# A graph network's count matrices: the first block read early into a buffer of its own, fewer tests on the counts, later tests on the lists

## The chip, the cores and the metric

The kernel runs on one core of one Trainium2 chip. The core has a matrix engine (PE, called TensorE), a vector engine (DVE), a scalar engine (ACT), a general engine (POOL), a queue engine that only issues transfers (SP), and 16 DMA engines that carry every transfer. The five instruction streams run side by side and wait for one another through semaphores. The metric is the device time of one execution in microseconds (us), as the median of several runs; lower is better.

## The reference

Two message-passing layers on a graph of 6250 nodes with 128 features and 200,000 edges sorted by target node. Cut to what matters:

```python
h = relu(layernorm(x))
agg_src  = segment_sum(h[src], dst, 6250)          # a node's sum over the sources of its edges
agg_edge = segment_sum(edge_attr_128, dst, 6250)
x = x + relu(concat([h, agg_src, agg_edge]) @ W.T + b)          # layer 0

h = relu(layernorm(x))
mean(h) = segment_sum(h[src], dst) / max(degree, 1)
h   = relu(mean(h) @ W1_l + b1 + h @ W1_r)                      # layer 1
out = relu(mean(h) @ W2_l + b2 + h @ W2_r)                      # layer 2
x = x + out
```

The targets are drawn as 6250 times the square of a uniform number, so the low node numbers have by far the most edges.

## The kernel before, in words

**Counts in place of gathers.** The kernel never gathers rows. It builds, once, the matrix of how many edges lead from each source to each target, and then each of the three layers is a product of that matrix with a table of features. The nodes are cut into NB = 49 blocks of 128. For a target block `b`, the counts are a tile `c` of 128 x (128 x 49) bf16 numbers, 1568 KB. They lie in DRAM in `counts_d`, block after block. The product for one target block is 49 matmuls, one for each source block, which accumulate in one PSUM tile `ps`. The table of features, `terms`, holds each number as a sum of three bf16 parts (NK = 3), so one matmul moves 384 columns, 385 in layer 0, where a column of ones counts the degree.

**The build (lines 486 to 587).** The edges come in 196 groups of 1024, in order of target. For each group DVE makes one-hot matrices (`sp`, `sq`, line 391), PE multiplies them (lines 534 and 546) and ACT puts the result in one of three ring buffers in SBUF (line 561). When a stretch of groups is done, SP writes the ring to `counts_d` (line 584, up to 1004 KB). The place of the write comes from the data, so two writes may overlap, and each waits until the one before has landed; the number of stretches is NS. Between these, PE also sums the edge features (line 437, into `aggE`, from `edge_t`, read on SP's queue at line 426) and multiplies the normed inputs by the weights of layer 0 (`products`, lines 336 to 352). At the end the build's buffers are released, and the pools `late` (tests, second table `terms1`), `loads` (three buffers of `c`) and `psum` take their place.

**The layers (lines 598 to 775).** `neighbours(layer, b)` reads `c` (line 603, SP's queue), multiplies (line 609; in layer 0 also `aggE` by `we_sb`, line 608), makes `rdeg`, one over the degree, in layer 0 (lines 611 and 612) and adds the three parts to `y` (line 620). In layers 0 and 1 the block's row of the next layer's table follows. In layer 0 that is the sum with `own` (line 740), the residual (741), the norm (326 to 334), and then, as in layer 1, a transpose `pt` on PE (line 341), a product `pz` (line 344) and the rounding into three parts (345 to 351). The table for the next layer must be whole before a block of that layer can finish, but its first 48 of 49 matmuls don't need the last block. A planner in the framework places each engine's instructions in one fixed order, from its own estimate of times; so `pt` of block b stands among the matmuls of block b + 1 at a place fixed in advance, and PE waits there if `h` isn't ready.

**The tests.** The fast path holds only for inputs that fit its windows, so the kernel tests them and computes all again in a slow, general way (`general`) if a test fails. There are three kinds. (1) No count may exceed 255, since bf16 holds integers exactly only so far: for each block, DVE takes the maximum of two halves of `c` (line 617) and reduces it (line 618); the even blocks do it in layer 0, the odd ones in layer 1. `worse` collects the results. (2) `windows_right` (lines 632 to 714) loads the list of targets twice, `both` and `nexts` (about 784 KB each, on POOL's queue), and tests windows and order on DVE; nothing but its loads holds these back. (3) Within it are tests on small tables, `rows` and `limits`: `limits` goes to DRAM and back (lines 660 and 662). `all_right` combines all in layer 2.

Of the kernel before, what the change touches and what calls it, by code (L numbers as in the profile page):

```python
# [9 lines left out]
F32 = mybir.dt.float32  # L10
F16 = mybir.dt.float16
BF16 = mybir.dt.bfloat16
I32 = mybir.dt.int32
AF = mybir.ActivationFunctionType
ALU = mybir.AluOpType
AX = mybir.AxisListType
# [4 lines left out]
P = 128  # L21
D = 128
# [6 lines left out]
NK = 3  # L29
# [27 lines left out]
def kernel(ctx: ExitStack, tc: tile.TileContext, x, srcl, dstl, edge, w0t, b0, w1l, b1, w1r, w2l, b2, w2r, out):  # L57
# [11 lines left out]
    nc = tc.nc  # L69
    N = x.shape[0]  # L70
    E = edge.shape[0]
    NB = -(-N // P)
# [16 lines left out]
    for g0, g1, *reg in regions:  # L89
        for g in range(g0, g1, reg[2]):  # L90
            stretches.append((g, min(reg[2], g1 - g), *reg))
    NS = len(stretches)

    dram = ctx.enter_context(tc.tile_pool(name="dram", bufs=1, space=bass.MemoryType.DRAM))
    counts_d = dram.tile([P, (NP + SWMAX) * NB], BF16, name="counts_d")
# [13 lines left out]
    work = fast.enter_context(tc.tile_pool(name="work", bufs=2))  # L109
    keep = fast.enter_context(tc.tile_pool(name="keep", bufs=1))  # L110
# [7 lines left out]
    rdeg = const.tile([P, NB], F32, name="rdeg")  # L118
    worse = const.tile([P, 6 + NC], F32, name="worse")
    bad = const.tile([1, 8], F32, name="bad")  # L120
    first = const.tile([P, 2, G], F32, name="first")
    terms = [keep.tile([P, NB, TW], BF16, name="terms0")]
    aggE = keep.tile([P, NP + WINMAX], F32, name="aggE")

    build = ExitStack()
    lists = build.enter_context(tc.tile_pool(name="lists", bufs=1))
# [8 lines left out]
    steps = lists.tile([1, GU - T1], F32, name="steps")  # L135
    seam_i = lists.tile([1, NS], I32, name="seam_i")
    NQ = max(w for _, _, _, w, *_ in regions) * NB
# [9 lines left out]
    far = once.tile([P, GU], F32, name="far")  # L147
    starts, seam, most = (once.tile([1, NS], F32, name=name) for name in ("starts", "seam", "most"))
    q_n = once.tile([P, GU], F16, name="q_n")
# [13 lines left out]
    si = 0  # L163
    for g0, g1, n, w, k, sw, win in regions:
        nc.gpsimd.memset(room[:, g0:g1], float(sw - w))
        m = -(-(g1 - g0) // k)
# [94 lines left out]
    for z, lay in ((p_n, p_e), (q_n, q_e)):  # L261
        for s0 in range(0, U, 2):
            pt = spsum.tile([P, 2, 256], F32, name="pt", bufs=2)
            for s in range(2):
                for u in range(U):
                    c = P * (s0 + s) - u + U - 1
# [11 lines left out]
    si = 0  # L278
    while si < NS:
        g0, k = stretches[si][:2]  # L280
        m = 1
        while si + m < NS and stretches[si + m][1] == k:
            m += 1
        units = unit[:, g0 : g0 + m * k].rearrange("o (m j) u -> o m (j u)", j=k)
        nc.vector.tensor_copy(starts[:, si : si + m], units[:, :, 0])
        if si == 0:
# [5 lines left out]
            op=ALU.subtract,  # L292
# [6 lines left out]
    nc.vector.memset(seam[:, 0:1], 0.0)  # L299
    nc.vector.tensor_tensor(seam[:, 1:], starts[:, 1:], starts[:, : NS - 1], op=ALU.subtract)  # L300
    nc.vector.tensor_tensor(seam[:, 1:], seam[:, 1:], most[:, : NS - 1], op=ALU.min)
    nc.vector.tensor_scalar(seam, seam, 0.0, float(NB), op0=ALU.max, op1=ALU.mult)
# [7 lines left out]
    for end, u in ((0, 0), (GU + 1, GU - 1)):  # L310
# [5 lines left out]
    nc.vector.tensor_scalar(  # L316
        bad[:, 1:2], starts[:, NS - 1 : NS], -1.0, float(NC * P - stretches[-1][5]), op0=ALU.mult, op1=ALU.add
    )
    setup.close()
    nc.gpsimd.memset(terms[0][:, :, NK * D :], 1.0)  # L320

# [56 lines left out]
    def value(ap, engine, most):  # L378
        return nc.values_load(
            ap, engines=[engine], min_val=0, max_val=most, skip_runtime_bounds_check_because="clamped on the chip"  # L380
        )
# [39 lines left out]
    def edge_sums(g):  # L421

        win = win_of(g)
        e = edges.tile([P, U, D], F32, name="edge_t")
        at_e = min(g * EG, E - EG)
        nc.sync.dma_start(e, edge[at_e : at_e + EG, :].rearrange("(p u) f -> p u f", u=U))
        hot = padded[g % len(padded)]
        nc.vector.tensor_tensor(  # L428
            hot[:, :, :win],
            iota[:, :win].unsqueeze(1).to_broadcast([P, U, win]),  # L430
            rel[:, g, :].unsqueeze(2).to_broadcast([P, U, win]),
            op=ALU.is_equal,
        )
        ps = bpsum.tile([P, 512], F32, name="pe", bufs=2)
        for u in range(U):
            behind = yield
            mm = nc.tensor.matmul(ps[:, :P], e[:, u, :], hot[:, u, :], start=u == 0, stop=u == U - 1)  # L437
            if behind is not None:
                tc.add_manual_dep(mm.ins, behind.name, IN_ORDER, reason="in turn with the counts")
        base = value(first_i[0:1, g : g + 1], ET.DVE, N - 1)  # L440
        to = aggE[:, bass.ds(base, win)]
        nc.vector.tensor_tensor(to, to, ps[:, :win], op=ALU.add)

    def all_edge_sums():
        for g in range(G):
            yield from edge_sums(g)

    edge_tiles = all_edge_sums()
    next(edge_tiles)
    summed = 0  # L450
# [42 lines left out]
    block = 0  # L493
    for i in range(2):
        load_chunk(i)
    for si, (g0, ng, n, w, k, sw, win) in enumerate(stretches):
        nq = NB * w
        ring = ring_of[si % 3]
# [5 lines left out]
        for g in range(g0, g0 + ng):  # L504
# [21 lines left out]
            for j in range(0, len(live), many):  # L526
                units = live[j : j + many]
                pu = bpsum.tile([P, 2 * 512], F32, name="pu", bufs=3)
                for i, t0 in enumerate(units):
                    for t in range(t0, t0 + n):  # L530
                        c = i * 512
                        while c < i * 512 + nq:
# [8 lines left out]
                            c = z  # L541
# [17 lines left out]
                for i, t0 in enumerate(units):  # L559
# [4 lines left out]
                    add = nc.gpsimd.tensor_tensor(to, to, fore[:, i, :], op=ALU.add)  # L564
# [15 lines left out]
        if si == 0:  # L580
            begin = 0
        else:
            begin = value(first_i[0:1, g0 : g0 + 1], ET.SP, N - 1) * NB
        nc.sync.dma_start(counts_d[:, bass.ds(begin, sw * NB)], ring[:, : sw * NB])
        before = ring
    assert block == NB and summed == GU and not writes
    build.close()
# [4 lines left out]
    loads = fast.enter_context(tc.tile_pool(name="loads", bufs=3))  # L592
# [4 lines left out]
    def neighbours(layer, b):  # L597

        ps = psum.tile([P, 512], F32, name="ps", bufs=3)
        m = NK * D + (layer == 0)  # L600
        products = []
        c = loads.tile([P, P, NB], BF16, name="c")
        nc.sync.dma_start(c, counts_d[:, b * P * NB : (b + 1) * P * NB].rearrange("p (d k) -> p d k", k=NB))
        for k in range(NB):
            products.append((c[:, :, k], terms[layer % 2][:, k, :m]))
        for i, (stands, moves) in enumerate(products):
            if layer == 0 and i == 1:
                nc.tensor.matmul(ps[:, :D], aggE[:, b * P : (b + 1) * P], we_sb, start=False, stop=False)
            nc.tensor.matmul(ps[:, :m], stands, moves, start=i == 0, stop=i == len(products) - 1)  # L609
        if layer == 0:  # L610
            nc.vector.tensor_scalar(rdeg[:, b : b + 1], ps[:, m - 1 : m], 1.0, None, op0=ALU.max)
            nc.vector.reciprocal(rdeg[:, b : b + 1], rdeg[:, b : b + 1])
        if b % 2 == layer:
            half = P // 2 * NB
            cf = c.rearrange("p d k -> p (d k)")
            high = late.tile([P, half], BF16, name="high")
            nc.vector.tensor_tensor(high, cf[:, :half], cf[:, half:], op=ALU.max)  # L617
            nc.vector.tensor_reduce(worse[:, 6 + b : 7 + b], high, AX.X, ALU.max)  # L618
        y = work.tile([P, D], F32, name="y", bufs=3)
        nc.vector.tensor_reduce(y, ps[:, : NK * D].rearrange("p (k f) -> p f k", k=NK), AX.X, ALU.add)  # L620
        return y

    def next_layer(layer, b, h):
# [9 lines left out]
    def windows_right():  # L633

        both = late.tile([P, 2, GU], F32, name="both")
        dst, far = both[:, 0], both[:, 1]
        nc.gpsimd.dma_start(dst.bitcast(I32), dstl)
        nexts = late.tile([P, GU], I32, name="nexts")
        nc.gpsimd.memset(nexts[P - 32 :, GU - U :], PAD)
        nc.gpsimd.dma_start(nexts[: P - 1, :], dstl[1:, :])  # L640
        nc.gpsimd.dma_start(nexts[P - 1 :, : GU - U], dstl[0:1, U:])
# [94 lines left out]
    for b in order:  # L736
        xt = load_x(b)
        r = load_own(0, b)
        y = neighbours(0, b)
        nc.vector.tensor_tensor(y, y, r, op=ALU.add)  # L740
        nc.vector.scalar_tensor_tensor(xt, y, 0.0, xt, op0=ALU.max, op1=ALU.add)
        nc.scalar.dma_start(x1_d[b * P : (b + 1) * P, :], xt)
        next_layer(1, b, normed(xt))


    def sage(layer, b):
        r = load_own(layer, b)
        y = neighbours(layer, b)
        nc.vector.scalar_tensor_tensor(y, y, rdeg[:, b : b + 1], r, op0=ALU.mult, op1=ALU.add)  # L749
        return y  # L750

    tests = windows_right()
    for b in order:
        next(tests, None)
        y = sage(1, b)
# [4 lines left out]
    for b in order:  # L760
# [8 lines left out]
        y = sage(2, b)  # L769
# [233 lines left out]
```

## The time and the profile before

| | us |
|---|---|
| median of 3 runs | 2244.61 (2238.09 to 2248.94) |
| the profiled execution, whole | 2237.15 |
| its span, first to last instruction | 2235.4 |
| PE busy in the span | 2073.7 (93%) |
| DVE busy | 1242.0 (56%) |
| build, to the last matmul that belongs to it | 911.4 |
| first matmul of layer 0 | 928.3 |
| maximum tests on `c` (lines 617 and 618), 49 of each, DVE | 87.6 and 167.5 |

The span is what the trace covers; the execution's own time has 1.75 us more around it. A timeline line gives the start, the duration (of a merged run of equal instructions), the engine, the line, the operation and, in brackets, how long the engine was idle before and what ended that. An engine's name with q (SPq, ACTq, POOLq) means that it issues a transfer there. The profiled execution is 0.33% under the median of the three runs.

### The profile page before, as it was taken

The numbers are of one execution on the slowest core, as the hardware profiler recorded it, in microseconds if no ns is written. First come the engines' busy times: TensorE is split into PE (matmuls) and PEld (weight loads), VectorE is DVE, ScalarE is ACT, GpSimd is POOL, SyncE is SP. The second block draws the span as 40 slices with busy tenths as digits, with TensorE's granted clock in tenths as the row PEclk, the third lists the DMA queues.
The fourth block names the chain that finished last, engine by engine and source line by source line (L and its number), as shares of the span: only waits on it lengthen the run. The fifth ranks groups of instructions, "written<-read, shape, count | busy, mean of one in ns | idle before, by whom it ended". The sixth has DMA issues, their size and how long they took to land.

```text
span 2235.4 us, 38803 instructions
## 1 busy us (share of the span) xinstructions
PE 2073.7 (93%) x13717; PEld 1691.1 (76%) x13717; DVE 1242.0 (56%) x2419; ACT 789.2 (35%) x2011; POOL 205.0 (9%) x427
## 2 busy tenths in 40 slices
PE   6977778899999999689999999999999999999998
PEld 5865567677776677478878887788888888888887
DVE  8987776577777777465555554544444431111111
ACT  3465566688888889211111111111111110000000
POOL 4576650000000000100000000000000000000000
PEclk9999999999999999899999999999999999999999
DMA  3555566678888778745555555555555556666663
GB/s 121 179 191 173 193 221 233 217 266 280 281 301 300 283 293 291 280 167 205 205 194 203 206 205 189 190 194 206 192 190 201 202 187 227 226 226 227 227 226 135
DMA packets 147226, 488.20 MB, mean 218 GB/s; under 512 B 16017, under 2 KB 86735, under 8 KB 127312
## 3 DMA queue, kind: packets, MB, share of 16 engines
q1 hardware_dynamic: 88452, 456.84, 56.9%
q10 hardware_dynamic: 57996, 27.16, 4.2%
q8 instruction: 111, 1.82, 0.3%
q0 software_dynamic: 576, 1.63, 0.2%
q14 instruction: 91, 0.75, 0.1%
HBM read 362.19 MB, written 123.38 MB: 217 GB/s over the span
## 4 chain that ended last, share of the span: by engine, by line
PE 60%; ACT 13%; DMA 9%; DVE 8%; issue 6%; ACTq 2%; POOLq 0%; SPq 0%; POOL 0%; DVEq 0%
PE ps L609 44%; ACT ring L561 10%; PE pe L437 6%; PE pu L534 5%; DMA counts_d<-ring 4%; DMA c<-counts_d 3%; PE pz L344 2%; ACTq L384 1%; DMA edge_t<-in_edge 1%; DVE sq L391 1%; DVE worse L618 1%; PE pt L341 1%; DVE high L617 1%; ACT h L334 1%; DVE sp L391 1%
## 5 line engine op out<-in xcount | busy, mean ns | idle before, releaser
L609 PE MATMUL ps<-terms,c 128*128 128x384 bf16 (+1 forms) x7203 | 1226.7, 327 | 16.9 <-DMA c<-counts_d 16.9
L609 PEld LDWEIGHTS <-c 128*128 128x128 bf16 x7203 | 1019.9, 142 | 183.6 <-issue 21.7
L437 PE MATMUL pe<-hot,edge_t 128*128 128x128 f32 x3136 | 521.0, 294 | 33.5 <-DMA edge_t<-in_edge 17.1
L561 ACT CAST ring<-pu 128x490 f32 (+6 forms) x891 | 469.5, 534 | 96.9 <-PE pu L546 43.0
L437 PEld LDWEIGHTS pe<-hot,edge_t 128*128 128x128 f32 x3136 | 418.2, 195 | 70.2 <-issue 18.1
L534 PE MATMUL pu<-sq,sp 128*128 128x512 bf16 (+7 forms) x1782 | 387.0, 313 | 55.9 <-ACT ring L561 26.7
L391 DVE TENSOR_TENSOR sq<-iota,q_e 128x3136 bf16<-128x3136 f16 (+8 forms) x196 | 353.5, 1804 | 102.4 <-PE pu L546 83.2
L620 DVE TENSOR_REDUCE y<-ps 128x128 f32<-128x384 f32 x147 | 81.2, 552 | 383.3 <-PE ps L609 383.3
L534 PEld LDWEIGHTS <-sp 128*128 128x128 bf16 x1782 | 175.6, 100 | 99.4 <-issue 33.6
L564 POOL TENSOR_TENSOR ring<-ring,fore 128x49 f32 x280 | 161.8, 578 | 102.3 <-ACT fore L556 36.1
L618 DVE TENSOR_REDUCE worse<-high 128x1 f32<-128x3136 bf16 x49 | 167.5, 3419 | 1.6
L546 PE MATMUL pu<-sc,sp 128*128 128x49 bf16 x892 | 163.1, 186 | 0.0
L347 DVE TENSOR_TENSOR r<-pz,b_sb 128x128 f32<-128x128 f32 x98 | 28.6, 292 | 225.0 <-ACT terms L345 225.0
L391 DVE TENSOR_TENSOR sp<-iota,p_e 128x1024 bf16<-128x1024 f16 x196 | 135.4, 691 | 21.8 <-PE pu L534 16.9
L546 PEld LDWEIGHTS <-sp 128*128 128x128 bf16 x892 | 87.0, 98 | 70.2 <-issue 38.5
L566 ACT CAST ring<-pu 128x196 f32 (+5 forms) x280 | 112.3, 403 | 67.9 <-issue 39.5
L330 ACT ACTIVATE rstd<-mv,eps 128x1 f32<-128x1 f32 x98 | 29.5, 301 | 291.1 <-DVE mv L328 291.0
L757 ACT ACTIVATE h<-y 128x128 f32<-128x128 f32 x49 | 15.2, 309 | 281.0 <-DVE y L749 281.0
L617 DVE TENSOR_TENSOR high<-c 128x3136 bf16<-128x3136 bf16 x49 | 87.6, 1789 | 42.1 <-DMA c<-counts_d 42.1
L428 DVE TENSOR_TENSOR hot<-iota,rel 128x64 f32<-128x64 f16 (+13 forms) x196 | 96.5, 493 | 0.0
L351 DVE TENSOR_TENSOR terms<-z,terms 128x128 bf16<-128x128 f32 x147 | 43.9, 299 | 59.5 <-ACT terms L350 59.0
L350 ACT CAST terms<-z 128x128 bf16<-128x128 f32 x147 | 44.0, 299 | 76.4 <-DVE z L349 75.6
(144 smaller groups left out, 867.3 us busy)
## 6 DMA issues: line engine op xcount, KB each, us to landing
c<-counts_d SPq DMA_DIRECT2D x147, 1568.0 KB, 6.1
edge_t<-in_edge SPq DMA_DIRECT2D x196, 512.0 KB, 4.2
counts_d<-ring SPq DMA_DIRECT2D x21, 735.0 KB, 3.8
counts_d<-ring SPq DMA_DIRECT2D x14, 1004.5 KB, 5.4
counts_d<-ring SPq DMA_DIRECT2D x14, 931.0 KB, 4.7
counts_d<-ring SPq DMA_DIRECT2D x14, 882.0 KB, 4.6
counts_d<-ring SPq DMA_DIRECT2D x14, 833.0 KB, 4.9
own<-r_d ACTq DMA_DIRECT2D x147, 64.0 KB, 5.3
```

The costliest lines, as they stand in the source:

```text
L391: nc.vector.tensor_tensor(to.rearrange("p t (c two) -> p t c two", two=2), iota[:, :m].rearrange("p (c two) -> p c two", two=2).unsqueeze( ...
L428: nc.vector.tensor_tensor(hot[:, :, :win], iota[:, :win].unsqueeze(1).to_broadcast([P, U, win]), rel[:, g, :].unsqueeze(2).to_broadcast([P ...
L437: mm = nc.tensor.matmul(ps[:, :P], e[:, u, :], hot[:, u, :], start=u == 0, stop=u == U - 1)
L534: mm = nc.tensor.matmul(pu[:, c:z], sp[:, t, :], sq[:, t, c - i * 512 : z - i * 512], start=t == t0, stop=t == t0 + n - 1 and (n > 1 or c ...
L546: mm = nc.tensor.matmul(pu[:, i * 512 : i * 512 + NB], sp_b[:, t, :], sc[:, slot + 1 - len(last_tiles) + j0, :NB], start=False, stop=j0 == ...
L561: nc.scalar.copy(ring[:, bass.ds(to_put[t0], nq)], pu[:, i * 512 : i * 512 + nq])
L564: add = nc.gpsimd.tensor_tensor(to, to, fore[:, i, :], op=ALU.add)
L566: put = nc.scalar.copy(ring[:, bass.ds(to_put[t0 // n] + NB, nq - NB)], pu[:, i * 512 + NB : i * 512 + nq])
L609: nc.tensor.matmul(ps[:, :m], stands, moves, start=i == 0, stop=i == len(products) - 1)
L617: nc.vector.tensor_tensor(high, cf[:, :half], cf[:, half:], op=ALU.max)
L618: nc.vector.tensor_reduce(worse[:, 6 + b : 7 + b], high, AX.X, ALU.max)
L620: nc.vector.tensor_reduce(y, ps[:, : NK * D].rearrange("p (k f) -> p f k", k=NK), AX.X, ALU.add)
```

## The change

Line numbers in the text are those of the kernel before.

1. **A buffer for block 0's counts.** A tile `c_early` is taken for the whole run. The write of stretch NS - 7 is followed, on POOL's queue, by a load of block 0's counts into it, while the last six writes (`EARLY` = NS - 6) are still to come. These six and the load are declared independent. A new entry of `bad` tests that stretch `EARLY` begins at or behind node 128; if it doesn't, all is computed again.
2. **Every fourth block uses it.** Blocks 0, 4, 8, ... 48 of each layer have their counts in `c_early`, the others in the three buffers of `loads`. All but block 0 of layer 0 are loaded on SP's queue as before.
3. **Fewer tests on the counts.** A count can't exceed its target's degree, so the degree (kept in `worse`) takes the place of the maximum over `c` for 48 blocks. Only block 0 keeps the two instructions; they are issued in layer 0 behind the sum of block 2.
4. **The lists wait.** Before the loads of `both` and `nexts`, POOL copies one column of `rdeg` into each tile: of block 12 and of block 16. So the loads can't begin before these blocks of layer 0 have their degrees. The loads of `rows` and `limits` have no such copy.

```diff
+    EARLY = NS - 6
+    c_early = keep.tile([P, P, NB], BF16, name="c_early")
...
+    nc.vector.tensor_scalar(
+        bad[:, 3:4], starts[:, EARLY : EARLY + 1], -1.0, float(P), op0=ALU.mult, op1=ALU.add
+    )
...
+    def load_counts(queue, c, b):
+        return queue.dma_start(c, counts_d[:, b * P * NB : (b + 1) * P * NB].rearrange("p (d k) -> p d k", k=NB))
...
-        nc.sync.dma_start(counts_d[:, bass.ds(begin, sw * NB)], ring[:, : sw * NB])
+        write = nc.sync.dma_start(counts_d[:, bass.ds(begin, sw * NB)], ring[:, : sw * NB])
+        if si >= EARLY:
+            tc.declare_no_dep(write.ins, group="early", reason="it begins behind the first block, or all is computed again")
+        if si == EARLY - 1:
+            tc.add_to_no_dep_group("early", load_counts(nc.gpsimd, c_early, 0).ins)
...
-        c = loads.tile([P, P, NB], BF16, name="c")
-        nc.sync.dma_start(c, counts_d[:, b * P * NB : (b + 1) * P * NB].rearrange("p (d k) -> p d k", k=NB))
+        c = c_early if b % 4 == 0 else loads.tile([P, P, NB], BF16, name="c")
+        if b or layer:
+            load_counts(nc.sync, c, b)
...
-            nc.vector.tensor_scalar(rdeg[:, b : b + 1], ps[:, m - 1 : m], 1.0, None, op0=ALU.max)
-            nc.vector.reciprocal(rdeg[:, b : b + 1], rdeg[:, b : b + 1])
-        if b % 2 == layer:
+            nc.vector.tensor_scalar(worse[:, 6 + b : 7 + b], ps[:, m - 1 : m], 1.0, None, op0=ALU.max)
+            nc.vector.reciprocal(rdeg[:, b : b + 1], worse[:, 6 + b : 7 + b])
+        y = work.tile([P, D], F32, name="y", bufs=3)
+        add = nc.vector.tensor_reduce(y, ps[:, : NK * D].rearrange("p (k f) -> p f k", k=NK), AX.X, ALU.add)
+        if layer == 0 and b == 2:
             half = P // 2 * NB
-            cf = c.rearrange("p d k -> p (d k)")
+            cf = c_early.rearrange("p d k -> p (d k)")
             high = late.tile([P, half], BF16, name="high")
-            nc.vector.tensor_tensor(high, cf[:, :half], cf[:, half:], op=ALU.max)
-            nc.vector.tensor_reduce(worse[:, 6 + b : 7 + b], high, AX.X, ALU.max)
-        y = work.tile([P, D], F32, name="y", bufs=3)
-        nc.vector.tensor_reduce(y, ps[:, : NK * D].rearrange("p (k f) -> p f k", k=NK), AX.X, ALU.add)
+            with tc.issue_after(add.ins):
+                nc.vector.tensor_tensor(high, cf[:, :half], cf[:, half:], op=ALU.max)
+                nc.vector.tensor_reduce(worse[:, 6:7], high, AX.X, ALU.max)
...
+        nc.gpsimd.tensor_copy(dst[:, 0:1], rdeg[:, 12:13])
         nc.gpsimd.dma_start(dst.bitcast(I32), dstl)
         nexts = late.tile([P, GU], I32, name="nexts")
+        nc.gpsimd.tensor_copy(nexts[:, 0:1], rdeg[:, 16:17])
```

## The prediction, on record before the changed kernel ran

> **What bounds the kernel now.** I read the page's busy times first, then PE's timeline at the seam from the build to layer 0 and at the end of layer 0, then SP's timeline at the seam, then the clock.
>
> ```profile
> PE 2073.7 (93%) x13717; PEld 1691.1 (76%) x13717; DVE 1242.0 (56%) x2419; ACT 789.2 (35%) x2011; POOL 205.0 (9%) x427
> ...
> L618 DVE TENSOR_REDUCE worse<-high 128x1 f32<-128x3136 bf16 x49 | 167.5, 3419 | 1.6
> ```
>
> PE is the bound. The 255 us of count tests (167.5 here, 87.6 at line 617) are DVE time; they are worth only what PE waits for them. PE's timeline, seam and end of layer 0:
>
> ```profile
> 928.32 0.51 PE L609 MATMUL ps<-terms,c 128*128 128x385 bf16 x1 [16.88 <-DMA c<-counts_d]
> 928.62 0.64 PE L608 MATMUL ps<-we_sb,aggE 128*128 128x128 f32 x2
> ...
> 939.00 0.38 PE L608 MATMUL ps<-we_sb,aggE 128*128 128x128 f32 x2
> ...
> 947.31 0.38 PE L608 MATMUL ps<-we_sb,aggE 128*128 128x128 f32 x2
> ...
> 955.54 0.47 PE L341 MATMUL pt<-ident,h 128*128 128x128 f32 x1 [7.69 <-ACT h L334]
> ```
> ```profile
> 1356.47 0.38 PE L608 MATMUL ps<-we_sb,aggE 128*128 128x128 f32 x2
> ...
> 1365.45 0.38 PE L608 MATMUL ps<-we_sb,aggE 128*128 128x128 f32 x2
> ...
> 1368.94 0.33 PE L341 MATMUL pt<-ident,h 128*128 128x128 f32 x1 [0.29 <-ACT h L334]
> ...
> 1374.95 0.39 PE L608 MATMUL ps<-we_sb,aggE 128*128 128x128 f32 x2
> ...
> 1388.07 0.38 PE L608 MATMUL ps<-we_sb,aggE 128*128 128x128 f32 x2
> ...
> 1405.03 0.33 PE L341 MATMUL pt<-ident,h 128*128 128x128 f32 x1 [2.18 <-ACT h L334]
> ```
>
> Each L608 marks a block of layer 0. See three things. (a) Two large holes, 16.88 and 7.69 us: the first waits for block 0's counts, the second for DVE, which sat 22.33 us at line 667 for the list `both` and then ran tests. (b) The first block takes 939.00 - 928.62 = 10.4 us, the second 8.3: after a hole PE runs slow, which costs 2.1 us. (c) Odd blocks take 8.98 us, even ones 9.43 to 9.50. In an even block `pt` comes after 18 matmuls, where `h` isn't quite ready (0.29 us idle, about 0.45 in all); in an odd one, where the planner allowed for the test, it comes after 32 and waits for nothing. The last interval, 13.12, and one near 1120 (10.94) are disturbed by tests: 6.1 us together.
>
> SP's timeline:
>
> ```profile
> 903.28 14.62 SPq L584 DMA_DIRECT2D counts_d<-ring  x4
> 921.52 26.14 SPq L603 DMA_DIRECT2D c<-counts_d  x5
> ```
>
> The last writes follow one another at landing (the one of 891.63 landed 7.0 us later, the next was issued at 898.77); only at 921.52 can counts be read. The page's issues give 6.1 us for a count load to land.
>
> [...] PEclk is 0.50 from 926 to 931. [...] `own`, 64 KB, needs 5.3 us beside a count load, `xt` 1.8. [...]
>
> **Part by part**, against the profiled execution (2237.15 us). I also read the order in which the changed program's instructions stand on each engine.
>
> *The seam.* The early load is behind the write issued at 885.30, so it starts near 890.5. DMA moved 332, 277, 240 and 344 GB/s in the four stretches of 5 us from 885: 1.57 MB at that mean, 298 GB/s, is up to 5.3 us taken from the write chain, and nothing if it fits the holes; I take 3.5. Block 0 then runs right after the build, hidden before the last write lands. Block 1's counts still wait for all writes: it starts where block 0 did, at 928.3 + 3.5 = 931.8, and cold (10.4): block 2 at 942.2. PE reaches `pt` of block 1 3.4 us later, at 945.6. Ahead of block 1's chain on DVE now stand the tests of `rows` and `limits` (lines 702 to 714). Their loads start at 922.2 + 3.5 on POOL; 2.0 us for four issues and 1.5 for 42 memsets bring `limits_d` to 929.3; it lands 6.2 later (as in the trace), `limits` 2.1 to 6.2 after that, `rows<-nothing` 1.5 to 6 after the test that precedes it: DVE is free at 940 to 949, I take 943. The chain from `ps` to `pt` is 3.45 us (1365.49 to 1368.94), so PE waits about 1 (0 to 7). Block 2 ends at 952.2. Block 2's chain then carries the one count test left, 1.8 + 3.4 us, and its `pt` stands after 45 matmuls: 1 us more. Block 4's counts go into `c_early`, which that test reads: their load is issued near 955.2, behind block 6's load, and the second of two loads landed 12.0 us after issue at the seam; I take 963.5, 1.3 us late. Block 4 starts at 963.5, before at 976.3: **12.8 us gained** (6 to 20).
>
> *Layer 0, blocks 4 to 48.* Without tests the planner puts every `pt` after 18 matmuls, except at blocks 13 (33) and 17 (27). So 22 blocks go from 8.98 to 9.43: +9.9; the disturbed 6.1 are gone; with roundings +3. The lists: `both` is issued 1.6 us after block 12's end (`rdeg` in 1.0, then POOL), behind block 16's count load of 6.1; it lands near 8.5. DVE waits there in order, then needs 5.2 us (lines 667 to 686: 934.04 to 940.80, less a count test of 1.8 between), and is free 13.7 after block 12's end, 4.3 later than block 13's. With 2.5 us more of tests inside it, the chain is ready 10.2 after block 13's end; PE arrives at 5.7: it waits 4.5 (0 to 6), and is cold for 2. `nexts` takes two landings in turn; the chain of block 17 with 2.3 us of tests makes PE wait 1.6 (0 to 6), cold 0.7. Less 0.9 for the two blocks' own waits: +8. **11 us lost** (3 to 17).
>
> *The layer boundaries.* 48 is a multiple of 4, so block 48 and block 0 of the next layer use the same buffer in turn. The order of SP has the reload of `c_early` waiting for PE's last matmul of block 48, and PE's order puts nothing but `pt` and `pz` of block 48 (0.7 us of work; 8.98 against 8.31) before block 0. Wait 0.2, land 6.1, start 0.1: 6.4 - 0.7 = 5.7 idle, and 2.1 cold: 7.8. Before, these loads came three blocks ahead; the boundary to layer 1 lost 2.2 at 1405.03, the one to layer 2 nothing over 0.5. **13.4 lost** (8 to 15).
>
> *Edits at nothing.* Degrees into `worse`, one test in `bad`, two small copies on POOL: DVE and POOL have room. The tests of odd blocks in layer 1 go without gain: there `pt` came after 46 matmuls and PE never waited. Layer 1's new place, after 9, was kept without a wait in the blocks without tests. Layer 2 is untouched. The planner's order within the build shifts a little: -3 to +3, I take nothing.
>
> *Sum:* -12.8 + 11 + 13.4 = +11.6: 2248.8 on the profiled execution, which lay 0.33% under the median; on the median 2244.61 + 11.6 = **2256**. About 0.5% (11.2 us) is what a measurement of this kernel can tell from no change.
>
> **Rivals.** *No change, by the seam paying in full:* the early load fits the holes between writes (3.5 back), `limits` and block 4 are not late (3.3 back) and the lists wait less (4 back): +0.8, 2245. For it: DMA stands at 63% busy from 895 to 900. Against: the chain of writes has no slack from 891 on. Chance 0.24. *Faster, not slower, by one mechanism:* the lists, moved beyond the rush, are hidden; if `both` lands within 4 us of block 12's end in place of 8.5 and `nexts` alike, the 8 us of list stalls are nil, and with the full seam the boundaries alone remain: 3 + 13.4 - 20 = -4, and -12 only with warm boundaries and a build 3 us shorter: 2233. It decides from where `both` lands before DVE comes to it. Against: `both` took 11.2 us in the trace. Chance 0.07. *Much slower:* every small transfer falls behind a count load: `limits` and `nothing` at the late end (+6), `nexts` (+4): 2266; or the early load does not do what it says and waits for the last writes, so block 0 starts where it did: +9, 2265. For it: `own` at 5.3. Against the second: the load's wait list names five transfer semaphores, and the order puts it ahead of the last memset of a ring. Chance 0.21. The forecast, 2250 to 2264: 0.48.
>
> **How the numbers follow.** Of the forecast's 0.48, 0.29 lies over 0.5% and 0.19 within; no change gives 0.20 within and 0.04 faster; faster 0.07; much slower 0.21. So slower 0.50, same 0.39, faster 0.11. The range, with 0.1 left out at each end, is 2242 to 2270; the forecast's own is 2250 to 2264.
>
> **What would show it.** Right: block 0 starts within 4 us of the build's end; a hole of 6 to 12 us before block 1; two holes near 5 us, with `c_early` as releaser, at the layer boundaries, PEclk 0.50 behind each; blocks of layer 0 at 9.4 us; a hole at `pt` in block 14. Wrong: a count load at the boundaries that is issued earlier; blocks at 9.0; no hole at block 14; a build that ends over 4 us elsewhere.

## The result, and the profile after

| | before | after |
|---|---|---|
| median, us | 2243.78 (6 runs, 2238.09 to 2248.94) | 2265.02 (6 runs, 2256.35 to 2270.46) |
| ratio after to before, 95% interval | | 1.0095 (1.0075 to 1.0115) |
| the profiled execution, us | 2237.15 | 2270.46 |
| issue of the ninth write to `counts_d` before the last | 874.98 | 888.00 |
| from there to the start of block 4 of layer 0 | 101.3 | 87.2 |
| blocks 4 to 48 of layer 0, start to start | 411.8 | 431.7 |
| from the start of block 48 to the end of the span | 847.3 | 861.8 |

The changed kernel is slower by 21.2 us on the medians. The two profiled executions differ by more, 33.3 us, because the profile before is of an execution that was faster than all six runs of its kernel, and the profile after of the slowest of its six. The table tells where: up to the ninth write before the last, which lies ahead of the early load and of all that follows, the profile after is 13.0 us later; from there to the end it is 20.4 us longer (-14.1 + 19.9 + 14.5, rounded), nearly the medians' difference. So I read every kernel below from that write on. Over the twelve profiles of this study it lies anywhere between 875.0 and 888.0. In e11_before_late_transpose, which changes nothing ahead of layer 0, it lies at 883.3, 8.3 us later than in the kernel before; so much comes without any edit of the build.

Lines are now those of the changed kernel: 621 and 622 are the matmuls of a block (608 and 609 before), 346 is `pt`, 454 a load of counts, 592 a write of counts, 685 and 712 the first tests of `both` and `nexts`. The page of the changed kernel, busy times, one group and one row of the transfers:

```profile
PE 2092.4 (92%) x13717; PEld 1696.2 (75%) x13717; DVE 999.7 (44%) x2324; ACT 791.9 (35%) x2011; POOL 204.4 (9%) x430
...
L622 PE MATMUL ps<-terms,c_early 128*128 128x384 bf16 (+1 forms) x1911 | 335.2, 329 | 6.0 <-DMA c_early<-counts_d 4.8
...
c_early<-counts_d SPq DMA_DIRECT2D x38, 1568.0 KB, 6.2
```

DVE has 242 us less to do, and it is of no use: PE, the bound, is busy for 19 us more with the same instructions. Part of that is the clock: in the two traces PE is busy for 72.6 us at half clock after and for 47.8 before, and half of the difference, about 12 us, is an estimate of what it costs. Where the rest comes from stays open. PE's timeline of the changed kernel at the seam, at blocks 13 and 17 and at the two layer boundaries:

```profile
929.63 0.32 PE L622 MATMUL ps<-terms,c_early 128*128 128x385 bf16 x1 [1.19 <-ACT ring L569]
...
941.62 0.33 PE L346 MATMUL pt<-ident,h 128*128 128x128 f32 x1 [3.52 <-ACT h L339]
...
944.51 0.52 PE L622 MATMUL ps<-terms,c 128*128 128x385 bf16 x1 [1.40 <-issue]
...
975.02 0.38 PE L622 MATMUL ps<-terms,c_early 128*128 128x385 bf16 x1 [0.19 <-DMA c_early<-counts_d]
...
1081.76 0.47 PE L346 MATMUL pt<-ident,h 128*128 128x128 f32 x1 [4.88 <-ACT h L339]
...
1126.88 0.47 PE L346 MATMUL pt<-ident,h 128*128 128x128 f32 x1 [6.79 <-ACT h L339]
...
1419.65 0.33 PE L346 MATMUL pt<-ident,h 128*128 128x128 f32 x1 [3.38 <-ACT h L339]
...
1422.40 10.67 PE L622 MATMUL ps<-terms,c_early 128*128 128x384 bf16 x49 [1.10 <-DMA c_early<-counts_d]
...
1865.84 4.38 PE L622 MATMUL ps<-terms,c_early 128*128 128x384 bf16 x13 [3.51 <-DMA c_early<-counts_d]
```

Block 0 now starts 1.19 us after the build, where the kernel before had a hole of 16.88. In exchange there are two new holes in layer 0, of 4.88 and 6.79 us, and one at each layer boundary. Behind the first boundary, where the granted clock is 0.50 from 1421 to 1426 us, 49 matmuls take 10.67 us; in e2_rotate, where no hole precedes them, 46 in a row take 7.69 to 7.70. Why the two holes of layer 0 are there is shown on DVE, POOL and SP, in that order:

```profile
1071.64 0.98 DVE L685 CAST both<-both 128x1568 f32<-128x1568 int32 x1 [4.24 <-DMA both<-in_dst]
...
1122.70 0.51 DVE L712 TENSOR_TENSOR both<-both,nexts 128x196 f32<-128x196 f32 x1 [6.30 <-DMA nexts<-in_dst]
```
```profile
1107.28 0.54 POOL L658 DMA_DIRECT2D nexts<-in_dst  x1 [0.30 <-POOL nexts L656]
1107.81 0.50 POOL L659 DMA_DIRECT2D nexts<-in_dst  x1
1117.16 0.51 POOL L664 DMA_DIRECT2D nexts<-in_dst  x1 [8.85 <-DMA nexts<-in_dst]
```
```profile
1105.98 0.33 SPq L454 DMA_DIRECT2D c_early<-counts_d  x1
...
1116.93 0.42 SPq L454 DMA_DIRECT2D c<-counts_d  x1
```

DVE stands at a list's first test before the list has landed, and behind that test stand instructions on which the next `pt` depends: for `both` the sums of block 13, for `nexts` the residual and the norm of block 17. For `nexts` there are two landings in turn: line 664 loads one element into a place that line 659 has just written, so POOL waits 8.85 us; then the element is issued 0.23 us behind a load of counts on SP and needs 5.42 us itself.

### The profile page after: what moved, and what is told of

It is laid out like the page before. It is cut to its first block, busy times and chain, and to the rows that moved or that the text cites. A ratio compares the mean times of both kernels' runs of the same rounds, so it can differ in the third digit from the quotient of the medians.

```text
span 2268.8 us, 38691 instructions
## 1 busy us (share of the span) xinstructions
PE 2092.4 (92%) x13717; PEld 1696.2 (75%) x13717; DVE 999.7 (44%) x2324; ACT 791.9 (35%) x2011; POOL 204.4 (9%) x430
## 4 chain that ended last, share of the span: by engine, by line
PE 57%; ACT 13%; issue 12%; DMA 9%; DVE 5%; ACTq 2%; POOL 0%; POOLq 0%; DVEq 0%; SPq 0%
PE ps L622 42%; ACT ring L569 10%; PE pe L442 6%; DMA counts_d<-ring 6%; PE pu L542 5%; PE pz L349 2%; DMA edge_t<-in_edge 2%; ACTq L389 2%; PE pt L346 1%; DVE sq L396 1%; ACT h L339 1%; PE pu L349 1%; ACT ring L574 1%; DMA nexts<-in_dst 1%; ACT rstd L335 1%
## 5 line engine op out<-in xcount | busy, mean ns | idle before, releaser
L622 PE MATMUL ps<-terms,c 128*128 128x384 bf16 (+1 forms) x5292 | 909.0, 327 | 1.4 <-issue 1.4
L622 PEld LDWEIGHTS <-c 128*128 128x128 bf16 x5292 | 750.5, 142 | 125.3 <-issue 6.5
L442 PE MATMUL pe<-hot,edge_t 128*128 128x128 f32 x3136 | 525.4, 295 | 42.6 <-DMA edge_t<-in_edge 25.2
L542 PE MATMUL pu<-sq,sp 128*128 128x512 bf16 (+7 forms) x1782 | 391.8, 315 | 61.7 <-ACT ring L569 31.4
L622 PE MATMUL ps<-terms,c_early 128*128 128x384 bf16 (+1 forms) x1911 | 335.2, 329 | 6.0 <-DMA c_early<-counts_d 4.8
L622 PEld LDWEIGHTS <-c_early 128*128 128x128 bf16 x1911 | 271.1, 143 | 54.2 <-DMA c_early<-counts_d 6.3
L349 PE MATMUL pz<-w_sb,hT 128*128 128x256 f32 x196 | 69.6, 437 | 1.0 <-ACT hT L348 1.0
```

The lines of the kernel that those rows point to most:

```text
L349: nc.tensor.matmul(pz, hT, w_sb[layer], start=True, stop=True)
L542: mm = nc.tensor.matmul(pu[:, c:z], sp[:, t, :], sq[:, t, c - i * 512 : z - i * 512], start=t == t0, stop=t == t0 + n - 1 and (n > 1 or c ...
```

## The experiments

All runs, read in three parts from the ninth write before the last. The last column is the measured ratio less one, times the median of the kernel before in the same runs, with its interval; it should agree with the sum, which is of one profile.

| kernel | to block 4 | blocks 4 to 48 | block 48 to end | sum against before | by the ratio |
|---|---|---|---|---|---|
| before | 101.3 | 411.8 | 847.3 | | |
| after | 87.2 | 431.7 | 861.8 | +20.4 | +21 (17 to 26) |
| e2_rotate | 87.7 | 430.7 | 846.2 | +4.2 | +5 (2 to 9) |
| e3_lists_at_once | 99.2 | 418.5 | 860.8 | +18.1 | +22 (16 to 27) |
| e4_no_early_load | 96.6 | 427.6 | 861.5 | +25.2 | +28 (24 to 33) |
| e5_bound_alone | 104.0 | 414.9 | 845.4 | +3.9 | +5 (2 to 8) |
| e6_rotate_late_tests | 87.8 | 416.8 | 846.0 | -9.7 | -5 (-8 to -2) |
| e7_late_transpose | 86.2 | 399.4 | 848.4 | -26.4 | -28 (-34 to -21) |
| e8_pool_guard | 84.5 | 399.4 | 848.6 | -27.8 | -24 (-31 to -18) |
| e9_nexts_apart | 87.0 | 424.3 | 861.5 | +12.5 | +17 (11 to 23) |
| e10_earlier_load | 83.9 | 399.4 | 849.8 | -27.3 | -27 (-33 to -21) |
| e11_before_late_transpose | 100.2 | 400.1 | 848.4 | -11.7 | -9 (-12 to -5) |

**e2_rotate: the layer boundaries.**

```diff
-        c = c_early if b % 4 == 0 else loads.tile([P, P, NB], BF16, name="c")
+        c = c_early if (layer * NB + b) % 4 == 0 else loads.tile([P, P, NB], BF16, name="c")
```

> The changed kernel with one edit: the four count buffers turn with the running number of the block over all layers, so block 48 of a layer and block 0 of the next no longer share a buffer. Theory A (the changed kernel's +21 us over the kernel before is layer boundaries +14, list waits +14, transpose after 18 matmuls +10, less about 15 at the seam; the build adds little): both boundary holes shrink to about 2 and 0.5 us and behind them the clock is not lost, so 13 to 14 us less than the changed kernel, a ratio to the kernel before of 1.003 (1.001 to 1.005). Theory B (the early load and its new order slow the build by 12 us or more, the boundaries would be hidden by other waits anyway): the time stays within 5 us of the changed kernel, ratio 1.007 to 1.010, with the boundary holes replaced by others.

Measured: ratio 1.0023 (1.0007 to 1.0038), as theory A had it. PE's timeline of this kernel, the first boundary and the second:

```profile
1407.39 4.79 PE L622 MATMUL ps<-terms,c_early 128*128 128x385 bf16 x28
1412.02 3.27 PE L622 MATMUL ps<-terms,c 128*128 128x384 bf16 x19
1415.56 0.33 PE L346 MATMUL pt<-ident,h 128*128 128x128 f32 x1 [0.27 <-ACT h L339]
...
1850.45 11.79 PE L622 MATMUL ps<-terms,c 128*128 128x384 bf16 x71
```

Block 48's last matmul (385 columns) and the next layer's first (384) follow each other without idle time, and the transpose is taken in among them. From block 48 on the kernel is 15.6 us shorter than the changed one (861.8 to 846.2). So the whole loss at the boundaries is the shared buffer.

**e3_lists_at_once: no hold on the lists.**

```diff
-        nc.gpsimd.tensor_copy(dst[:, 0:1], rdeg[:, 12:13])
...
-        nc.gpsimd.tensor_copy(nexts[:, 0:1], rdeg[:, 16:17])
```

> The changed kernel without the two copies that hold the loads of the lists both and nexts back until blocks 12 and 16: the lists are read at the seam, as in the kernel before. Theory A: the holes before blocks 14 and 18 go (6.6 and 8.2 us, 14.8 in all), but VectorE waits for both at the seam with block 1's to 3's sums behind it, and block 4 starts 5 to 9 us later than in the changed kernel; net 6 to 10 us less, ratio to the kernel before 1.005 to 1.007. Theory C (holding the lists was right, the rush at the seam costs more than the two holes): block 4 starts more than 15 us later, ratio 1.010 or more. Theory B: no difference of the layer-0 part matters beside the build, ratio within 0.002 of the changed kernel's 1.0095.

Measured: ratio 1.0096 (1.0071 to 1.0122), above theory A's 1.005 to 1.007 and where theory B had put it, but not for B's reason: the parts of layer 0 do change, and cancel. Blocks 4 to 48 gain 13.2 us, and block 4 starts 11.9 us later, between the 5 to 9 of theory A and the 15 of theory C. DVE's timeline of this kernel, first test and first sum of block 1, and then PE's:

```profile
946.50 0.98 DVE L683 CAST both<-both 128x1568 f32<-128x1568 int32 x1 [4.70 <-DMA both<-in_dst]
...
961.24 0.14 DVE L625 TENSOR_SCALAR worse<-ps 128x1 f32<-128x1 f32 x1
```
```profile
965.29 0.47 PE L346 MATMUL pt<-ident,h 128*128 128x128 f32 x1 [9.19 <-ACT h L339]
```

The tests, once begun, go on for 14 us ahead of that sum; I had reckoned with the wait for the landing but not with all the tests in one piece behind it. Held or not, the lists cost about the same, at the seam or at blocks 14 and 18; the two ratios don't tell them apart.

**e4_no_early_load: the counts of block 0 behind the last write.** Both the early load and the declarations of independence are taken out:

```diff
-        if si == EARLY - 1:
-            tc.add_to_no_dep_group("early", load_counts(nc.gpsimd, c_early, 0).ins)
...
-        if b or layer:
-            load_counts(nc.sync, c, b)
+        load_counts(nc.sync, c, b)
```

> The changed kernel without the early load: block 0's counts come on SP behind the last write, into the same buffer, and all writes stay in their old order. Theory A: the write chain gets its 4 us back, but TensorE waits some 15 us behind the build for block 0's counts in place of reading them early; block 4 starts about 5 us later than in the changed kernel, counted from the end of the build: ratio to the kernel before 1.011 to 1.013. So of the seam's gain only a third is the early load's, the rest that the lists and count tests left the seam. Theory B (the early load slows the build): the build ends 12 us or more earlier than in the changed kernel and the ratio is 1.004 to 1.007.

Measured: ratio 1.0127 (1.0106 to 1.0148), where theory A put it, but its split of the seam was wrong. Block 4 starts 9.3 us later than in the changed kernel (87.2 to 96.6), so the early load earns 9.3 of the 14.1 us, and the rest of the change 4.7, not the other way round. Of that rest it is rather the lists than the count tests: with the count tests alone gone (e5_bound_alone), block 4 starts 2.7 us later than in the kernel before. The hole of this kernel on PE's timeline:

```profile
938.73 0.54 PE L617 MATMUL ps<-terms,c_early 128*128 128x385 bf16 x1 [16.15 <-DMA c_early<-counts_d]
```

**e5_bound_alone: degrees in place of maxima, and nothing else of the change, in the kernel before.**

```diff
-            nc.vector.tensor_scalar(rdeg[:, b : b + 1], ps[:, m - 1 : m], 1.0, None, op0=ALU.max)
-            nc.vector.reciprocal(rdeg[:, b : b + 1], rdeg[:, b : b + 1])
-        if b % 2 == layer:
+            nc.vector.tensor_scalar(worse[:, 6 + b : 7 + b], ps[:, m - 1 : m], 1.0, None, op0=ALU.max)
+            nc.vector.reciprocal(rdeg[:, b : b + 1], worse[:, 6 + b : 7 + b])
+        if layer == 0 and b == 0:
```

> The kernel before with one part of the change alone: every block but block 0 has its counts bounded by the degrees, so the count test stays for block 0 alone (no early load, no held lists, buffers as before). Theory A: VectorE loses about 250 us of work and TensorE gains nothing by it; the planner puts every transpose of layer 0 after 18 matmuls, where it waits 0.3 us, 22 blocks go from 8.98 to 9.43 (+10), the disturbed blocks near the end of layer 0 and at 1120 us go (-6), the second hole at the seam is 2 to 4 us shorter: ratio 1.000 (0.999 to 1.002). Theory D (tests taken from VectorE are a gain): ratio 0.997 or less. Theory E (the later transposes are the main loss): ratio 1.004 or more.

Measured: ratio 1.0023 (1.0011 to 1.0034), just above theory A's 0.999 to 1.002; a gain is excluded, and so is theory E's 1.004. Every block from 4 on takes 9.31 to 9.49 us, blocks 4 to 48 are 3.1 us longer, as worked out. The second hole at the seam is no shorter, 9.65 us against 7.69, which theory A had the other way.

**e6_rotate_late_tests: e2's buffers, and the lists' tests in layer 1.**

```diff
+        adds[layer, b] = add
...
-        next(tests, None)
+        with tc.issue_after(adds[(1, b - 1) if b else (0, NB - 1)].ins):
+            next(tests, None)
```

> The changed kernel with the count buffers turning over the layers (as in e2_rotate) and every VectorE test of the lists held behind layer 1's sums, one step to a block; the lists are loaded as in the changed kernel. Theory A (VectorE came to the lists before they had landed, and what stood behind it made the holes before blocks 14 and 18): both holes go, 14.8 us, and about 1 us at the seam with the tests of rows and limits; layer 1 has room for the tests. From the end of the build to the end of the kernel 1307 us (1305 to 1311) against e2_rotate's 1323.1; ratio to the kernel before 0.996 (0.994 to 0.998). Rival F (the loads themselves disturb the blocks beside them, or the tests make TensorE wait wherever they are): at least 8 of the 14.8 us come back, at blocks 14 and 18 or in layer 1, ratio 0.999 or more.

Measured: ratio 0.9978 (0.9966 to 0.9991), in theory A's range. Blocks 4 to 48 lose 13.9 us against e2 (430.7 to 416.8), and the blocks from 48 on nothing. PE's timeline of this kernel from the start of block 14, with block 13's `pt` in it, to the start of block 15:

```profile
1064.66 0.38 PE L622 MATMUL ps<-we_sb,aggE 128*128 128x128 f32 x2
...
1068.09 0.33 PE L346 MATMUL pt<-ident,h 128*128 128x128 f32 x1 [0.24 <-ACT h L339]
...
1074.11 0.38 PE L622 MATMUL ps<-we_sb,aggE 128*128 128x128 f32 x2
```

The loads are where they were; only the waiting instruction is gone from the path, and block 13's 4.88 us hole with it. Over the whole kernel the gain on e2 is about 10 us by the ratios, whose intervals also allow the 13.9 of the two profiles.

**e7_late_transpose: e6, and the transposes of layer 0 later.** Each block's `next_layer` is now called after the following block's matmuls, and held:

```diff
+        if b:
+            with tc.issue_after(marks[0, b].ins):
+                next_layer(1, b - 1, h)
...
-        next_layer(1, b, normed(xt))
+        h = normed(xt)
```

> As e6_rotate_late_tests, and in layer 0 each block's transpose is held behind the 25th matmul of the block after it. Theory A (at its place after 18 matmuls the transpose comes 0.3 us before h is ready, and costs 0.45 us a block in all): blocks of layer 0 take 8.98 us in place of 9.43, 44 blocks give 20 us, from the end of the build to the end 1287 us (1284 to 1292), ratio to the kernel before 0.987 (0.985 to 0.990). Rival G (the 0.45 us are a price of the transposes and of the smaller matmuls themselves, or TensorE then waits for the terms of the last block at the boundary): less than 6 us gained on e6_rotate_late_tests.

Measured: ratio 0.9877 (0.9848 to 0.9907), theory A. PE's timeline of this kernel, where line 623 marks a block:

```profile
1072.74 0.27 PE L346 MATMUL pt<-ident,h 128*128 128x128 f32 x1
1072.85 0.33 PE L624 MATMUL ps<-terms,c 128*128 128x385 bf16 x1
1073.01 0.38 PE L623 MATMUL ps<-we_sb,aggE 128*128 128x128 f32 x2
...
1082.10 0.38 PE L623 MATMUL ps<-we_sb,aggE 128*128 128x128 f32 x2
```

The planner placed the transpose behind all 49 matmuls, later than the hold asks. No idle time stands before it, and every block takes 9.09 us, not quite the 8.98 expected: 43 blocks at 0.34 less, 14.6, and block 4 (8.42 us against 10.83 in e6) make nearly all of the 17.4 us by which blocks 4 to 48 are shorter than in e6.

**e8_pool_guard and e10_earlier_load: what the early load and the order of the build cost.** In e8 one instruction of e7 moves to POOL, which brings back the order of before on PE and SP in the build; in e10 the early load moves forward as well. It was issued at 368.1 us, in e8 at 894.7.

```diff
-    nc.vector.tensor_scalar(
+    nc.gpsimd.tensor_scalar(
         bad[:, 3:4], starts[:, EARLY : EARLY + 1], -1.0, float(P), op0=ALU.mult, op1=ALU.add
```
```diff
-    EARLY = NS - 6
+    EARLY = 30
```

> As e7_late_transpose, with one small instruction moved: the guard of 1x1 written to bad[3] runs on POOL instead of VectorE, after which the order of the whole build is again that of the kernel before, with the early load in it. Theory A (the early load costs the build about 4 us and the changed order about 2, the rest of the 17 us between the two profiles is run-to-run): the build ends near 920 us, between 915 and 925, and the median is 0 to 4 us under e7_late_transpose's. Theory B (the changed order alone costs the build 8 us or more): the median is 8 us or more under e7_late_transpose's.

> As e8_pool_guard, with the early load of block 0's counts tied to write 29 in place of the sixth write from the end: it starts near 430 us, where DMA is half idle and POOL has nothing else. Theory A (the early load's price of 3.4 to 7 us, seen as a hole of 3.5 to 4.8 us in TensorE shortly before the build's end, is what it takes from the crowded end of the write chain): the hole goes, the last 2 per cent of the build take 16.4 us as in the kernel before instead of 21.0, and the median is 3 to 6 us under e8_pool_guard's ratio of 0.989, 0.986 to 0.988. Rival J (the build is bound by what DMA moves in all, wherever): the build loses the same 3 to 7 us near 430 us or after, the ratio stays at 0.989.

Measured: e8 0.9891 (0.9861 to 0.9921), not to be told from e7, so theory B is out, and the order of the build is worth nothing that these two runs can show; their intervals, of about 7 us either way, leave room for a few us. e10: 0.9879 (0.9853 to 0.9905), not to be told from e8, although its hole near the build's end did go. PE's timeline of e8, then of e10:

```profile
907.81 0.41 PE L542 MATMUL pu<-sq,sp 128*128 128x512 bf16 x2 [3.65 <-ACT ring L569]
...
934.78 0.36 PE L624 MATMUL ps<-terms,c 128*128 128x385 bf16 x1 [3.78 <-issue]
```
```profile
913.85 0.32 PE L624 MATMUL ps<-terms,c_early 128*128 128x385 bf16 x1 [1.37 <-ACT ring L569]
...
928.93 0.52 PE L624 MATMUL ps<-terms,c 128*128 128x385 bf16 x1 [6.61 <-DMA c<-counts_d]
```

The hole of 3.65 is gone in e10, and the hole before block 1 is 6.61 instead of 3.78. Block 1 needs the last write landed, and PE, finished sooner, only waits longer there. From the ninth write before the last to block 4 it is 84.5 and 83.9. My expectation took a hole on PE for a price; the price is what the chain of writes loses. From the ninth write before the last to the last it takes 44.6 in e8 and 42.9 in e10, so 1.7 us came back there in these two profiles, too little for the ratios to show.

**e9_nexts_apart: the one-element load without its wait.** The row of `nexts` is read only as far as the element; the columns left out are never used.

```diff
-        nc.gpsimd.dma_start(nexts[P - 1 :, : GU - U], dstl[0:1, U:])
+        nc.gpsimd.dma_start(nexts[P - 1 :, : GU - 2 * U], dstl[0:1, U : GU - U])
```

> The changed kernel with one load of the list nexts cut short, so that the one-element load of its last row no longer overlaps it and need not wait for it. Theory A (the hole before block 18 came from two landings one after the other, the second of one element behind a count load): the one-element load is issued with the others, VectorE has nexts 5 us or more earlier, and the hole before block 18 shrinks from 6.8 to between 0 and 2 us, block 18 from 17.6 to at most 12. Rival H (any small load at this place stands behind the count loads, whatever it waits for): the last of the loads of nexts still lands more than 12 us after block 16's end, and the hole stays above 4 us.

Measured: ratio 1.0076 (1.0050 to 1.0101), which the intervals don't tell from the changed kernel's; so the profile has to decide, at the one block concerned:

```profile
1113.63 0.33 PE L346 MATMUL pt<-ident,h 128*128 128x128 f32 x1 [3.20 <-ACT h L339]
```

Block 18 takes 14.07 us in place of 17.61, with a hole of 3.20, not 0 to 2: the wait was 3.5 of the 8.2 us that this block had lost. The element is now loaded at the seam (933.6). The remaining two loads of `nexts` (issued at 1098.8 and 1099.3) take 8.9 and 8.7 us and land 10.6 us after block 16's end, just before DVE's test of them starts at 1108.19, beside the count load issued 1.3 us earlier. So both theories hold a part: the second landing cost 3.5 us at this block, and the first is late by itself. Blocks 4 to 48 are 7.4 us shorter than in the changed kernel, but 3.3 of these lie at block 14 (12.75 us in place of 16.06), which the edit doesn't touch.

**e11_before_late_transpose: the kernel before with e7's edit alone.** Nothing of the change is in it.

> The kernel before with the transposes of layer 0 held behind the 25th matmul of the block after it, and nothing of the change. Theory A (0.45 us is lost wherever the transpose comes after 18 matmuls, tests or not): the blocks of layer 0, 8.98 and 9.43 us in turn, all take about 9.09 us as in e7_late_transpose, the two disturbed blocks go too, blocks 4 to 48 take 400 us in place of 412, ratio 0.995 (0.993 to 0.997). Rival K (with the count tests on VectorE the transposes meet them elsewhere): 404 us or more, ratio 0.998 or more.

Measured: ratio 0.9962 (0.9948 to 0.9977), theory A. PE's timeline of this kernel, where line 609 marks a block:

```profile
1065.30 0.39 PE L609 MATMUL ps<-we_sb,aggE 128*128 128x128 f32 x2
...
1074.39 0.38 PE L609 MATMUL ps<-we_sb,aggE 128*128 128x128 f32 x2
```

Every block from 4 on takes 9.09 us, with all count tests on DVE as before. What held layer 0 back was the place of `pt`, not DVE's load. The kernels that have this, the change, e2's buffers and e6's tests together, e7, e8 and e10, are the fastest here: 24 to 28 us under the kernel before by their ratios, and so 46 to 49 under the changed one.

## Why the prediction came out as it did

The forecast said slower, 2256, with 2242 to 2270 around it; the median is 2265.0. That is inside the wide range and 1 us outside the forecast's own 2250 to 2264. The sign and the mechanisms were right, the size half: +11.6 worked out, +20.4 in the profile.

- *The early load takes 3.5 us from the write chain:* the last write is issued 46.1 us after the ninth before it, 42.6 in the kernel before. 3.5 measured. That it agrees to the tenth is luck, since 3.5 was picked between nothing and 5.3 (5.4 with the load's 1568 KB as 1.61 MB). The size holds, though: over the profiles it takes 44.6 to 47.1 us with the early load among these writes, 41.7 to 43.4 without.
- *The seam gains 12.8:* 14.1. Block 1 was to start at 931.8 on the old profile's clock, 56.8 after the ninth write before the last, and does at 56.5; block 2 at 67.2, and does at 67.5. Not foreseen was the 3.52 us hole before block 0's own `pt`; it is hidden by the wait for block 1's counts. `pt` of block 1 waits 0.28, not 1, and block 4 waits 0.19 for its counts, not 1.3.
- *Blocks of layer 0, +3:* +3.1 in e5, which has this alone; +5.1 in the changed kernel (19.9 less the two list stalls).
- *The lists, +8:* this is the term that was mis-sized. `both` came out right in this profile, with some luck: block 14 takes 16.06 us, 6.6 over its neighbours, against 4.5 + 2. In e4 and e9, with the same instructions there, it takes 12.84 and 12.75. In e9 the hole is 3.54 us in place of 4.88, and the granted clock stays at 1.00 from 1070 to 1082; in the changed kernel it is 0.50 from 1080 to 1086. `nexts` was given 1.6 + 0.7 and costs 8.2 (block 18, 17.61). I had counted two landings in turn but not that the second, of one element, would be issued right behind a load of counts; e9 and POOL's timeline show it. The profile before had shown it: at the seam this same load, issued at 935.1 with a load of counts still under way (332 GB/s moved from 931 to 936), took 7.8 us; the forecast left that out. The credit of 0.9 was not there to take.
- *The boundaries, +13.4:* +14.5 by the table, all of it removed by e2.
- *Edits at nothing, the order of the build included:* e7 against e8 shows no difference beyond their intervals.

So 5.9 of the 8.8 us missed are `nexts`. I had listed this very collision under the rival "much slower", with +4, and the time came out at that rival's 2265; its other members, `limits` late and a load that waits for the last writes, did not happen. Of the signs named beforehand two came in pieces (the hole before block 1 as 3.52 and 1.40 us around `pt`, those at the boundaries as 3.38 and 1.10, and 1.44 and 3.51), so the hole before block 1 was under the 6 to 12 named. And one of the signs of being wrong did come: the build ends 17 us from its old place in the profile, 13.0 of them before the early load begins. I take most of these for run-to-run, since the rest alone gives 20.4 of the medians' 21.2, and e11 has 8.3 of them with no edit there. A few us may yet be the build's changed order: the ninth write before the last lies at 878.2 on average in the five profiles with the old order on PE and at 884.7 in the seven with the new one. The medians don't show it: the last column of the table above exceeds the sum by 2.0 us on average with the old order and by 2.4 with the new. This stays open.

## What to carry to other kernels

A buffer set aside for an early transfer must not enter a rotation in which its last use in one phase meets its first in the next: count modulo over all phases. When work leaves an engine that isn't the bound, look at where the planner then puts the bound's instructions, and set the place by hand: here that alone gave about 9 us with all count tests in place, while removing the tests alone cost about 5. Once the place was set, blocks 4 to 48 took 400.1 us with the tests and 399.4 without. A load that is held back only helps if the instruction that reads it is held back by more than the load's landing time beside the traffic of that phase, here 8.4 us for `both`.

## What the runs showed of the hardware that was not expected

**An idle time of about the same length went once with a full clock and once with a halved one.** Stretches of e9: start and end, length, PE busy with its instructions, granted clock, DMA share, GB/s. The first two lie around block 13's hole of 3.54 us, the last two behind block 17's of 3.20.

```profile
1072.00:1074.00 2.00, 0.00 (x0) 1.00 0.17 56
1074.00:1076.00 2.00, 0.85 (x5) 1.00 0.12 33
...
1114.00:1115.50 1.50, 1.50 (x6) 0.63 0.22 64
1115.50:1117.00 1.50, 1.50 (x6) 0.50 0.16 45
```

The longer hole left the granted clock at 1.00; behind the shorter one it was 0.50, from 1114.39 to 1117.80, for 3.41 us. In the traces of the kernel before and of the changed one the granted clock changes 23 and 37 times, each time at a whole multiple of 3.41 us from the other changes of its trace. Divided at such places, the 3.54 us hole of e9 falls into two stretches, in which PE is busy for 1.58 and 1.69 of 3.41 us, and most of the 3.20 us hole into one, in which it is busy for 0.76. So these two holes differ by their place far more than by their length.

The traces of the kernel before and of the changed one divided like this give 1257 stretches at full clock. After each of the 24 in which PE was busy for under 0.4 of the time the clock was halved; from 0.4 to 0.5 after 6 of 7, from 0.5 to 0.6 after 1 of 20, and from 0.6 on after none of 1206. Of their stretches at half clock, none of 17 with PE busy under 0.8 was followed by full clock, and the one from 0.8 to 0.9 and all 28 above were. Busy is PE's matmuls as the profile has them, with modelled ends. One stretch at half clock, filled with work, costs 1.7 us by estimate, half of its 3.41 us; so the 2 us for a cold clock in my sums is an average over one or two stretches, or none.

**Transfers of one element and of 0.2 KB took about as long as one of 1568 KB when they were issued just behind one.** The one element of `nexts`, issued 0.23 us behind a load of 1568 KB in the changed kernel, took 5.4 us. At the seam of the kernel before, with a load of counts and the long one of `nexts` still under way, it took 7.8. `limits_d` there, 0.2 KB issued 0.08 us behind a load of counts, took 6.2, and `limits`, again 0.2 KB, issued at 945.88 with a DMA share of 0.05 from 945.8 to 948.1, took 2.1. In layer 0 of the changed kernel `both` and the long load of `nexts` (784 and 778 KB), each issued 1.30 us behind a load of 1568 KB, took 8.4 and 8.9 us, and the row of 6.1 KB in `nexts` 9.1, while a load of 1568 KB takes 6.2 by the profile's page.
